# A graph layer's kernel: the node group that is not full comes first, the last groups' products may end behind the last edge tiles, and a piece of the node table per two edge tiles

## The chip, the core and the metric

The kernel runs on one core of a Trainium2 chip. A core has five engines with a program each: PE (TensorE, matrix products), DVE (VectorE), ACT (ScalarE), POOL (GpSimd) and SP (SyncE, which here only issues transfers). They run at the same time and wait for each other by semaphores; each works through its own program in order. Matrix products land in PSUM, everything else on the chip is in SBUF, and transfers (DMA) go between SBUF and the memory outside, HBM. The metric is the time of one launch on the device in microseconds (us).

## What is computed

There are 12500 nodes with 256 features, and 212500 edges, sorted by their target node, each of one of 8 types. Every node has an edge to itself.

```python
h = jnp.maximum(_layernorm(x, axis=-1), 0.0)
hx = jnp.einsum('ni,rio->rno', h, weight)            # 8 weights of 256 x 256
msg = hx[edge_type, src]
agg = jax.ops.segment_sum(msg, dst, num_segments=num_nodes)
node_repr = agg * ALPHA ** 0.5 + h_bias + (h @ loop_weight) * (1.0 - ALPHA) ** 0.5
x = x + node_repr
```

## The kernel before

The kernel sums first and multiplies afterwards: for each target node and type it sums the rows h of the sources, and multiplies these eight sums by the eight weights.

**Edge tiles.** The edges are cut into 802 units, each of two tiles of up to 128 edges (1603 tiles, NT). A unit of blocks 1 and later takes 267 edges; the self edges, each the last of its node's, are taken out of it and treated apart. 128 units are a block (b = 0 to 6). For each tile POOL gathers the 128 source rows from HBM into `msg` (`gather`, L687, its transfer at L704), 58 tiles ahead (AHEAD); some odd tiles are fetched row by row by the queues of SP and ACT instead (L715). DVE makes a one-hot matrix `oh` of (node in a window of 22, type) for four tiles at once (L732). PE multiplies `msg` by `oh` into a PSUM bank `ps` (`edge_sums`, L759), one bank per unit and four banks in all, and DVE adds the bank into `acc` (`add_sums`, L771), one unit later.

**The ring.** `acc` is a ring of 6 x 128 node columns (RING = 768, SLOTS = 6 groups of GROUP = 128) with 8 types each. Where a unit's window lies in it is computed on the chip from its first node: `places` (L581) counts how often the ring has turned by then (`wraps`, L982) and the result is loaded into DVE's registers for 16 units at a time (`load_offsets`, L740, whose DVE load the trace shows at L743), in every 32nd tile.

**Groups.** 128 nodes in order are a group (98 of them; the last has 84 nodes). When the unit that surely holds a group's last edge has been added (`plan.last`), the group's work is put into a queue: eighteen products (L923: the self product with `wl`, then two halves for each of eight types; each product is two passes on PE) into one of two PSUM tiles `po`, and then `finish` (L931), in which DVE adds `x` and the bias and the result (L934, L935), and SP stores it. Four groups (XG) share a tile of rows that is loaded (`load_groups`, L871) and stored at once. A freed slot of the ring is cleared (`clear`, L781) or started with the self edges' terms (`begin`, L806). For the latter, `mark` (L820) and its followers find the type of each node's self edge from the blocks that may hold it (`plan.blocks`).

**The order.** The order of every engine's program is written out by hand in the loop over tiles (L1070 to L1133). In each tile it issues: the gather for 58 tiles on, two single-row fetches per queue, a block's index preparation when it is due (`blocks_ahead`, L1041, in tile 256 b - 184: SP loads the indices, and DVE works on them in the same and the following tiles, its first instruction on them being L381), the rest of what an earlier tile began (`after`), then the edge products, waiting background work, group products from the queue, and the sums of the unit before. The queue's pace comes from a due time: an item has a tile from which it may be issued (`ready`) and one by which it shall be (`until`, L1122), and every tile takes so much from the front that all will be kept.

**The head.** The normalised table h must first be written to HBM: 26 pieces of up to 512 rows are loaded (L672), normalised in `moments` (L644: DVE's statistics, ACT's root at L653, DVE's reciprocal and shift, ACT's activation at L661) and stored (L681), all transfers on SP. Four pieces are begun ahead of the loop. Until the table is there, tiles gather raw rows of x and normalise their messages in the same way, four tiles (BATCH) at once. In the loop (L1079 to L1094) every fourth tile begins a batch of messages and each of the other three begins one piece. When the last piece is done, `norms_end` (L1035) loads the weights, which ACT scales six tiles later (L1031, L1032), and gathers of tiles from 58 + 8 on read h. No group's work is queued before the weights are scaled.

Of the kernel before, what the change touches and what calls it, by code (L numbers as in the profile page):

```python
# [75 lines left out]
class Plan:  # L76
# [7 lines left out]
    def __init__(self, N, E):  # L84
        U = PAIR * P
        first = P * U
        self.NU = NU = -(-E // U) if E <= first else P + -(-(E - first) // EDGES)
        self.EU = E - (NU - 1) * U if E <= first else E - first - (NU - P - 1) * EDGES
        self.NT = NU * PAIR - (1 if self.EU <= P else 0)
        self.rate = N / E * EDGES  # L90
        s = 6.5 * (E / 4) ** 0.5 + EDGES

        lines = [(U, 0), (EDGES, first - P * EDGES)]
        last = (1.1 * EDGES, 1.1 * (first - P * EDGES) - 0.1 * E - 1.5 * EDGES + s)
        self.low = [(a * N / E, (b - s) * N / E) for a, b in [*lines, last]]
        self.high = [(a * N / E, (b + s) * N / E) for a, b in lines]
        self.starts = list(range(0, N, GROUP))
        self.ends = self.starts[1:] + [N]
        self.NG = len(self.starts)
        self.last = [  # L100
            min([NU - 1, *(int((e + 2 - b) / a) + 1 for a, b in self.low)]) for e in self.ends]
        self.last[-1] = NU - 1
        self.first = [
            max(0, min(int((s - WIN - 2 - b) / a) for a, b in self.high) - 1) if s else 0
            for s in self.starts]

        self.blocks = [
            [k for k in range(1, -(-NU // P))
             if max(a * P * k + b for a, b in self.low) <= e + 2
             and max(a * min(NU - 1, P * k + P - 1) + b for a, b in self.high) + WIN + LASTS + 2 >= s]  # L110
            for s, e in zip(self.starts[::XG], self.starts[XG::XG] + [N])]
        self.typed = min([q for q, b in enumerate(self.blocks) if b], default=len(self.blocks))
        assert XG * self.typed >= SLOTS
# [102 lines left out]
def kernel(  # L216
# [48 lines left out]
    ones_b = const.tile([P, P], BF16, name="ones_b")  # L265
    zero = const.tile([P, 1], F32, name="zero")
    flag = const.tile([1, 1], I32, name="flag")
    NK = -(-N // RING)
    wraps = const.tile([P, NK], F32, name="wraps")

    def place_of(t):
# [4 lines left out]
    with ExitStack() as main:  # L276
# [304 lines left out]
        def places(b, got):  # L581

            def wraps_():
                got["wrapped"] = small.tile([P, NK], F32, name="wrapped")
                nc.vector.tensor_scalar(
                    got["wrapped"], wraps, got["base"][:, 0:1], None, op0=ALU.is_lt)

            def turns():
                got["turns"] = small.tile([P, 1], F32, name="turns")
                nc.vector.tensor_reduce(got["turns"], got["wrapped"], AX.X, ALU.add)  # L590

            def position():
                got["pos"] = small.tile([P, 1], F32, name="pos")
                nc.vector.scalar_tensor_tensor(
                    got["pos"], got["turns"], float(-RING), got["base"][:, 0:1],
                    op0=ALU.mult, op1=ALU.add)

            def turn():
                pt = ps_d.tile([P, 512], F32, tag="pt", name="ptr")
                nc.tensor.transpose(pt[0:1, :P], got["pos"], ident)  # L600
                place[b] = small.tile([1, P], I32, name="offs")
                nc.vector.tensor_copy(place[b], pt[0:1, :P])

            return [wraps_, turns, position, turn]
# [266 lines left out]
        def load_groups(name, table, q):  # L871

            if XG * q >= plan.NG:
                return
            d0, d1 = plan.starts[XG * q], plan.ends[min(plan.NG, XG * (q + 1)) - 1]
            full, rest = divmod(d1 - d0, P)
            rows_ = got[name, q] = rowp.tile([P, XG, D], F32, tag="rows", name=f"{name}r")
            if full:
                nc.sync.dma_start(
                    rows_[:, :full, :],  # L880
                    table[d0 : d0 + full * P].rearrange("(k p) d -> p k d", p=P))
            if rest:
                nc.sync.dma_start(rows_[:rest, full, :], table[d0 + full * P : d1])

        def group_ahead(g):

# [23 lines left out]
        def group_work(g):  # L910

            d0, n = plan.starts[g], plan.ends[g] - plan.starts[g]
            s0 = g % SLOTS * GROUP
            first_dep = [True]

            def product(r, c):
                if (r, c) == (R, 0):
                    got["out", g] = outs[g % 2][:, 0, :]
                if r == R:
                    lhs, rhs = got["self", g][:, c, :n], wl[:, c, :]  # L920
                else:
                    lhs, rhs = acc[:, c, r, s0 : s0 + n], w[:, c, r * D : (r + 1) * D]
                i = nc.tensor.matmul(got["out", g][:n], lhs, rhs, start=(r == R and c == 0),  # L923
                                     stop=(r == R - 1 and c == KC - 1))
                if (r, c) == (R, 0) and g < 2:
                    tc.add_manual_dep(i.ins, done["bias"], SYNC_DEP, reason="one engine at a time")
                if r < R and first_dep[0]:
                    first_dep[0] = False
                    tc.add_manual_dep(i.ins, added[plan.last[g]].name, SYNC_DEP, reason="sums complete")

            def finish():  # L931
                q, k = divmod(g, XG)
                rows_ = got["x", q]
                nc.vector.tensor_add(rows_[:n, k, :], rows_[:n, k, :], outs[g % 2][:n, 1, :])  # L934
                nc.vector.tensor_add(rows_[:n, k, :], rows_[:n, k, :], got["out", g][:n])  # L935
                if XG * (q + 1) >= plan.NG:
                    nc.sync.dma_start(out[d0 : d0 + n], rows_[:n, k, :])
                elif k == XG - 1:
                    first = plan.starts[XG * q]
                    nc.sync.dma_start(  # L940
                        out[first : d0 + n].rearrange("(k p) d -> p k d", p=P), rows_)
                b = g + SLOTS
                q, k = divmod(b, XG)
                if b < plan.NG:
                    if q < plan.typed:
                        clear(b)
                    else:
                        begin(b)
                if q + 1 >= plan.typed and XG * (q + 1) < plan.NG:
                    if k == XG // 4:  # L950
                        load_groups("h", h32, q + 1)
                    if k == XG - 2:
                        mark(q + 1)
                    if k == XG - 1:
                        done["late"].append((done["tile"] + REST, lambda: find_types(q + 1)))
                        done["late"].append((done["tile"] + 2 * REST, lambda: spread_types(q + 1)))

            def last():
                done["late"].append((done["tile"] + REST, finish))

            work = []
            for r in [R, *range(R)]:
                for c in range(KC):
                    work.append((0.55, lambda r=r, c=c: product(r, c)))
            work.append((0.0, last))
            return work

        with tc.manual_schedule():
# [10 lines left out]
            tid = small.tile([P, NB], I32, name="tid")  # L979
            nc.gpsimd.iota(tid, pattern=[[P, NB]], base=0, channel_multiplier=1)  # L980
            for k in range(NK):
                nc.gpsimd.memset(wraps[:, k : k + 1], (k + 1) * RING - 0.5)  # L982
            nc.vector.memset(eps, EPS)
            nc.vector.memset(ones, 1.0)
            nc.vector.memset(ones_b, 1.0)
# [84 lines left out]
            for t in range(NT):  # L1070
# [7 lines left out]
                after = []  # L1078
                if t % BATCH == BATCH - 1:  # L1079
                    after = batch(t + 1 + BATCH)  # L1080
                elif done["norm"] < len(pieces):
                    for i in range(1 if NT > 400 else 20):
                        if done["norm"] < len(pieces):
                            after.append(norm_rows(done["norm"]))
                            done["norm"] += 1
                    if NT <= 400:
                        for f in after:
                            f()
                        after = []
                    if done["norm"] == len(pieces):  # L1090
                        for f in after:
                            f()
                        after = []
                        norms_end(t)  # L1094
# [19 lines left out]
                while waiting and (len(waiting) > LAG or t == NT - 1):  # L1114
                    u, ps = waiting.pop(0)
                    add_sums(u, ps)
                    while (next_group < plan.NG and plan.last[next_group] <= u
                           and (done["weights"] or (NT <= 400 and done["norm"] == len(pieces)))):
                        g = next_group
                        while background and NT <= 400:  # L1120
                            background.pop(0)[1]()
                        until = PAIR * (plan.first[g + SLOTS] - 3) - REST if g + SLOTS < plan.NG else NT - 1  # L1122
                        ready = t + max(0, min(DELAY, NT - 1 - t - 2 * DELAY))
                        until = max(ready, min(until, ready + int(GROUP / plan.rate * PAIR)))
                        if g and g % SLOTS == 0:
# [44 lines left out]
```

## Time and profile before

| what | before |
|---|---|
| median of 3 runs | 2582.19 us (2568.44, 2582.19, 2586.18) |
| profiled execution | 2603.5 us, its span 2601.8 us |
| mean granted clock of PE | 0.889 |
| PE, POOL, DVE, ACT busy | 1956.1, 1491.8, 1322.9, 219.5 us |
| gathers from x, from h | 96, 1475 |
| first, last gather from h begins | 178.8, 2519.4 us |
| tile 8, 28, 40, 56 begins on PE | 100.8, 158.5, 189.3, 212.3 us |
| tile 72, 96, 120, 1602 begins on PE | 236.4, 277.3, 306.9, 2586.4 us |
| last store issued | behind 2597.6 us |

The profile is of one execution, and its engines' busy times are sums over a span in which several work side by side. PE's matmuls are pipelined, so the distance from one start to the next says more than a duration. A tile's four passes on PE are those of L759; the n-th tile's start was counted off from them. "Idle before" names what ended an engine's wait; the word issue there means that no wait for another engine is seen.

### The profile page before, as it was taken

What the parts mean: (1) busy time and instruction counts of PE and PEld (TensorE: products, weight loads), DVE (VectorE), ACT (ScalarE), POOL (GpSimd) and SP (SyncE); (2) the same over time, 40 slices, a digit from 0 to 9 for tenths busy, and PEclk for the clock granted to TensorE, in tenths of its full rate; (3) what the DMA queues carried; (4) which work ended last, traced back from release to release, by engine and by line L of the source; (5) the groups of instructions that cost most, each with busy time, mean ns of one, the idle gap of its engine ahead of it and who ended that gap; (6) DMA issues with size and microseconds to landing.
All of it is one profiled execution on the core that took longest, in us unless ns stands there. A gap on an engine that the chain in (4) does not pass through costs nothing. (4 is left out here: it accounts for less than half of the span.)

```text
span 2601.8 us, 42363 instructions
## 1 busy us (share of the span) xinstructions
PE 1956.1 (75%) x10411; PEld 1733.3 (67%) x10411; DVE 1322.9 (51%) x3281; ACT 219.5 (8%) x470; POOL 1491.8 (57%) x1597
## 2 busy tenths in 40 slices
PE   0248887876788777878777777878688787787888
PEld 0237776775677666767666676767577676676778
DVE  3577644455645344754444744444745444744453
ACT  3564100000000000000000000000000000000000
POOL 7435666655566565566566565666466665565640
PEclk9558989988989898889998898999798998898999
DMA  6682433333333333233333233333333333333320
GB/s 198 203 280 83 121 90 115 106 92 110 96 96 106 99 105 111 86 112 104 94 114 110 84 105 109 96 104 98 96 106 94 114 104 86 108 106 92 111 79 13
DMA packets 153661, 282.02 MB, mean 108 GB/s; under 512 B 31709, under 2 KB 103140, under 8 KB 153412
## 3 DMA queue, kind: packets, MB, share of 16 engines
q0 software_dynamic: 75408, 206.01, 27.4%
q1 hardware_dynamic: 73908, 71.16, 8.7%
q10 hardware_dynamic: 4096, 2.11, 0.3%
q8 instruction: 86, 1.41, 0.2%
q14 instruction: 163, 1.34, 0.2%
HBM read 253.55 MB, written 25.60 MB: 107 GB/s over the span
## 5 line engine op out<-in xcount | busy, mean ns | idle before, releaser
L704 POOL DMA_INDIRECT msg<-h,gidx x1475 | 1398.9, 948 | 943.2 <-issue 359.0
L759 PE MATMUL ps<-oh,msg 128*128 128x176 f32 (+1 forms) x6412 | 1235.0, 323 | 384.3 <-issue 246.2
L759 PEld LDWEIGHTS ps<-oh,msg 128*128 128x128 f32 x6412 | 1117.9, 208 | 532.2 <-issue 307.5
L923 PE MATMUL po<-w,acc 128*128 128x256 f32 x3136 | 959.8, 406 | 51.1 <-issue 50.4
L923 PEld LDWEIGHTS po<-w,acc 128*128 128x128 f32 x3136 | 574.4, 204 | 116.9 <-issue 92.3
L732 DVE TENSOR_TENSOR oh<-fixed,cols 128x704 f32<-128x704 f32 x402 | 355.5, 885 | 512.0 <-remote 242.1
L771 DVE TENSOR_TENSOR acc<-acc,ps 128x352 f32 x802 | 412.9, 515 | 346.6 <-PE ps L759 159.5
L814 DVE SCALAR_TENSOR_TENSOR acc<-types,pst 128x256 f32<-128x256 bf16 (+1 forms) x688 | 234.7, 414 | 148.5 <-remote 99.1
L802 ACT ACTIVATE self_t<-pst 128x256 f32<-128x256 f32 x98 | 37.4, 382 | 1984.3 <-DMA msg<-h 810.3
L704 POOL DMA_INDIRECT msg<-in_x_dram,gidx x96 | 90.9, 947 | 84.6 <-issue 60.8
L923 PE MATMUL po<-wl,self_t 128*128 128x256 f32 x392 | 113.6, 409 | 16.6 <-issue 12.5
L923 PEld LDWEIGHTS po<-wl,self_t 128*128 128x128 f32 x392 | 72.9, 206 | 30.5 <-issue 21.5
L840 PE MATMUL ptt<-loops,mark 128*128 128x24 bf16 x216 | 9.3, 177 | 94.3 <-ACT self_t L802 59.5
L840 PEld LDWEIGHTS <-mark 128*128 128x128 bf16 x216 | 9.0, 100 | 97.9 <-issue 97.7
L661 ACT ACTIVATE xt<-xt,n_shift,n_rstd 128x256 f32<-128x256 f32 x98 | 50.9, 589 | 21.2 <-DVE n_shift L658 6.9
L661 ACT ACTIVATE msg<-msg,e_shift,e_rstd 128x256 f32<-128x256 f32 x96 | 49.8, 589 | 17.2 <-DVE e_shift L658 6.0
L795 PE MATMUL pst<-ident,hr 128*128 128x128 f32 x196 | 42.3, 293 | 10.6 <-issue 8.1
L934 DVE TENSOR_TENSOR xr<-xr,po 128x256 f32<-128x256 f32 x98 | 40.4, 412 | 19.1 <-remote 11.5
L935 DVE TENSOR_TENSOR xr<-xr,po 128x256 f32<-128x256 f32 x98 | 41.2, 421 | 3.4
L356 DVE TENSOR_SCALAR moves<-fixed 128x267 int32<-128x267 int32 x84 | 36.3, 432 | 1.6
L858 ACT ACTIVATE diagonal<-ident,kinds 128x128 bf16<-128x128 f32 x88 | 28.1, 390 | 104.8 <-DVE kinds L855 42.9
L795 PEld LDWEIGHTS pst<-ident,hr 128*128 128x128 f32 x196 | 27.9, 152 | 13.5 <-issue 10.4
(201 smaller groups left out, 382.8 us busy)
## 6 DMA issues: line engine op xcount, KB each, us to landing
msg<-h SPq DMA_DIRECT2D x2048, 1.0 KB
msg<-h ACTq DMA_DIRECT2D x2048, 1.0 KB
msg<-h,gidx POOLq DMA_INDIRECT x1475
xt<-in_x_dram SPq DMA_DIRECT2D x24, 512.0 KB
h<-xt SPq DMA_DIRECT2D x24, 512.0 KB
xr<-in_x_dram SPq DMA_DIRECT2D x24, 512.0 KB
hr<-h SPq DMA_DIRECT2D x24, 512.0 KB
out_dram<-xr SPq DMA_DIRECT2D x24, 512.0 KB
```

Of the source, the lines that this page charges most:

```text
L356: nc.vector.tensor_single_scalar(m, packed, 1 << (bit + k), op=ALU.bitwise_and)
L661: nc.scalar.activation(rows_[j], rows_[j], AF.Relu, bias=shift[:n, j : j + 1], scale=rstd[:n, j : j + 1])
L704: nc.gpsimd.indirect_dma_start(out=msg[t], out_offset=None, in_=table[:, :], in_offset=bass.IndirectOffsetOnAxis(ap=gidx[b][:, at : at + 1 ...
L732: nc.vector.tensor_tensor(o[:, k : k + v, :i, :], iota_f.unsqueeze(1).unsqueeze(1).to_broadcast([P, v, i, C]), of.unsqueeze(3).to_broadcas ...
L759: nc.tensor.matmul(ps[:, c, from_ : from_ + width], m[:, c * P : (c + 1) * P], o[:, :width], start=(i == 0 and c == 0), stop=(end and c == ...
L771: i = nc.vector.tensor_tensor(a, a, ps, op=ALU.add)
L795: nc.tensor.transpose(pst[:, c, :n], rows_[:n, c * P : (c + 1) * P], ident[:n, :n])
L802: i = nc.scalar.activation(got["self", g][:, :, :n], pst[:, :, :n], AF.Copy)
L814: i = nc.vector.scalar_tensor_tensor(acc[:, :, r, s0 : s0 + n], of, float(r + 1), pst[:, :, :n], op0=ALU.is_equal, op1=ALU.mult)
L923: i = nc.tensor.matmul(got["out", g][:n], lhs, rhs, start=(r == R and c == 0), stop=(r == R - 1 and c == KC - 1))
L934: nc.vector.tensor_add(rows_[:n, k, :], rows_[:n, k, :], outs[g % 2][:n, 1, :])
L935: nc.vector.tensor_add(rows_[:n, k, :], rows_[:n, k, :], got["out", g][:n])
```

## The change

Three things are done. First, the group of 84 nodes becomes group 0 (nodes 0 to 83), and all later groups are full: every boundary moves by `pad` = 44 nodes. In the ring, node d stands at (d + 44) mod 768, so group 0 takes columns 44 to 127. `wraps_` and `position` compute that place with the same number of instructions. The first four groups' rows are loaded in two transfers and stored group by group; the last two are loaded in one. Second, the groups whose products have no later slot to clear are due at tile NT + 2 and not at NT - 1. Third, a piece of the node table is begun in every even tile that begins no batch, so in two of four tiles, and not in three of four.

```diff
-        self.starts = list(range(0, N, GROUP))
+        self.pad = -N % GROUP
+        self.starts = [0, *range(GROUP - self.pad, N, GROUP)]
...
-    NK = -(-N // RING)
+    NK = -(-(N + plan.pad) // RING)
...
                 nc.vector.tensor_scalar(
-                    got["wrapped"], wraps, got["base"][:, 0:1], None, op0=ALU.is_lt)
+                    got["wrapped"], wraps, got["base"][:, 0:1], float(-RING),
+                    op0=ALU.is_lt, op1=ALU.mult)
...
                 nc.vector.scalar_tensor_tensor(
-                    got["pos"], got["turns"], float(-RING), got["base"][:, 0:1],
-                    op0=ALU.mult, op1=ALU.add)
+                    got["pos"], got["turns"], float(plan.pad), got["base"][:, 0:1],
+                    op0=ALU.add, op1=ALU.add)
...
-            d0, d1 = plan.starts[XG * q], plan.ends[min(plan.NG, XG * (q + 1)) - 1]
-            full, rest = divmod(d1 - d0, P)
+            gs = range(XG * q, min(plan.NG, XG * (q + 1)))
             rows_ = got[name, q] = rowp.tile([P, XG, D], F32, tag="rows", name=f"{name}r")
-            if full:
+            first = gs[0]
+            if plan.ends[first] - plan.starts[first] < P:
                 nc.sync.dma_start(
-                    rows_[:, :full, :],
-                    table[d0 : d0 + full * P].rearrange("(k p) d -> p k d", p=P))
-            if rest:
-                nc.sync.dma_start(rows_[:rest, full, :], table[d0 + full * P : d1])
+                    rows_[: plan.ends[first], 0, :], table[: plan.ends[first]])
+                first += 1
+            k = first - gs[0]
+            if k < len(gs):
+                nc.sync.dma_start(
+                    rows_[:, k : len(gs), :],
+                    table[plan.starts[first] : plan.ends[gs[-1]]].rearrange("(k p) d -> p k d", p=P))
...
-            s0 = g % SLOTS * GROUP
+            s0 = (d0 + plan.pad) % RING
...
-                if XG * (q + 1) >= plan.NG:
+                if q == 0 or XG * (q + 1) >= plan.NG:
                     nc.sync.dma_start(out[d0 : d0 + n], rows_[:n, k, :])
...
-                nc.gpsimd.memset(wraps[:, k : k + 1], (k + 1) * RING - 0.5)
+                nc.gpsimd.memset(wraps[:, k : k + 1], (k + 1) * RING - plan.pad - 0.5)
...
                 if t % BATCH == BATCH - 1:
                     after = batch(t + 1 + BATCH)
-                elif done["norm"] < len(pieces):
+                elif t % 2 == 0 and done["norm"] < len(pieces):
...
-                        until = PAIR * (plan.first[g + SLOTS] - 3) - REST if g + SLOTS < plan.NG else NT - 1
+                        until = PAIR * (plan.first[g + SLOTS] - 3) - REST if g + SLOTS < plan.NG else NT + 2
```

## The prediction

> **What bounds the kernel now.** I read the page's busy table and slices first, then the three stretches head, middle and tail, then the chain at the end. The profiled execution took 2603.5 us (span 2601.8); the median of the three runs shown is 2582.2, so the sum below is made on the trace and its difference is then taken off the median.
>
> ```profile
> PE   0248887876788777878777777878688787787888
> DVE  3577644455645344754444744444745444744453
> POOL 7435666655566565566566565666466665565640
> PEclk9558989988989898889998898999798998898999
> ```
>
> No engine is full in the middle; PE is nearest, at 7 to 8 tenths. The first three slices (195 us) are another stage: PE is nearly idle there, and its clock is at 0.5. The same stage by stretches (columns: us, busy us of PE, weight load, DVE, ACT, POOL, granted clock, DMA share):
>
> ```profile
> 100.80:172.00 71.20, 32.33 (x104) 28.00 (x104) 55.43 (x255) 58.54 (x124) 22.67 (x24) 0.50 0.90 297
> 172.00:189.30 17.30, 6.18 (x25) 5.65 (x25) 7.95 (x29) 7.66 (x12) 7.56 (x8) 0.60 0.91 290
> 236.40:277.30 40.90, 28.70 (x150) 24.85 (x150) 35.77 (x114) 15.50 (x28) 25.80 (x27) 0.87 0.31 88
> 2519.40:2603.00 83.60, 37.26 (x216) 34.44 (x216) 0.99 0.07 22
> ```
>
> (The last line is of the edge products, L759, alone.) From 100.8 to 172 ACT is busy 82% and DVE 78%: they normalise the node table and the first messages in turn, and this is the bound there. From 172 to 189 ACT waits for the weights. From 236 to 277 DVE is busy 87%, because the messages that are still raw are normalised beside the index work of block 1. After POOL's last gather (2519.4) PE has 216 passes of edge products left, 54 tiles, and works without a gap: the tail.
>
> ```profile
> 138.20 2.07 ACT L661 ACTIVATE xt<-xt,n_shift,n_rstd 128x256 f32<-128x256 f32 x4 [0.44 <-DVE n_shift L658]
> 140.18 0.28 ACT L653 ACTIVATE n_rstd<-n_mv,eps 128x4 f32<-128x4 f32 x1
> 141.28 2.08 ACT L661 ACTIVATE xt<-xt,n_shift,n_rstd 128x256 f32<-128x256 f32 x4 [0.82 <-DVE n_rstd L657]
> 143.98 2.07 ACT L661 ACTIVATE xt<-xt,n_shift,n_rstd 128x256 f32<-128x256 f32 x4 [0.44 <-DVE n_shift L658]
> ...
> 146.69 1.09 ACT L661 ACTIVATE msg<-msg,e_shift,e_rstd 128x256 f32<-128x256 f32 x2 [0.44 <-DVE e_shift L658]
> ```
>
> The head's cadence: every group of four rows, a piece of the table (xt) or a batch of messages (msg), costs 2.7 us on the ACT-DVE round trip, 3.1 once in four tiles (the one-hots get in). Three pieces and one batch per four tiles are 11.2 us.
>
> ```profile
> 2586.43 0.76 PE L759 MATMUL ps<-oh,msg 128*128 128x176 f32 x4
> 2588.68 1.06 PE L923 MATMUL po<-wl,self_t 128*84 128x256 f32 x4 [1.49 <-DVE xr L935]
> 2589.58 7.07 PE L923 MATMUL po<-w,acc 128*84 128x256 f32 x32
> ```
>
> The end: after the last tile PE waits 1.49 us, then does 36 passes of the last group's products.
>
> **The change part by part**
>
> *A. Half the pieces per tile.* Before, pieces go on three of four tiles, so the 22 that are left when the loop starts end at tile 28; after, on two of four, at tile 42. Messages are gathered raw for tiles up to the end of the pieces + 58 + 8: 96 before, 108 after, so three more batches. In time: batch 8 has one piece fewer ahead of it, 100.2 - 2.7 = 97.5. Then nine rounds of four tiles at 2 pieces + 1 batch = 8.5 us, two of them with a clear (0.9 more): 78.3. The two short pieces end it at 181.8, against 172.0. So the table ends 10 us later, but PE's supply is at tile 48 and not at 34. The weight loads are queued on SP behind the last stores, and their scaling ended 16.0 us after the table (188.0 - 172.0): 197.8 after. Tiles up to 55 need nothing behind that scaling, so PE begins tile 56 at about 199.1; before, it began tile 40 at 189.3. No group's products have been done at either point: both wait for the scaled weights.
>
> Then the catching up. A pass of an edge product is 0.15 us apart (0.6 a tile), one of a group product 0.215, 36 to a group.
> Tiles 56 to 72: before 24.1 us (16 x 0.6 + 36 x 0.215 + 6.4 of stall while DVE loads its registers, L743). After, groups 0 and 1 both fall here (order of the built program: 56 to 62, 62 to 71): 7.7 more, 31.8; at tile 72 after stands at 230.9, before at 236.4.
> Tiles 72 to 96: before 40.8, DVE bound; after 24 more passes, 5.2 us of PE, of which I put 2 on the path, since PE idles 12 us there.
> Tiles 96 to 120: before 29.7. After, 12 of these tiles are raw too. A raw tile makes DVE's load about 1.7 us (from the 40.8 for 24 tiles) where the others go by in 1.25: +5; 14 group passes fewer: -3, partly hidden: +3 net.
> Sum at tile 120: 230.9 + 42.8 + 32.7 = 306.4, against 306.9: **-0.5 us**. The trace doesn't show this mix. Bounds: if PE's own work set the pace from tile 56, 64 x 0.6 + 180 x 0.215 + 13 for two register loads = 90, tile 120 at 289, -18; if none of the lead is kept and the later end of the table and three batches count whole, 10 + 5 = +15. I take the value by stretches, nearest to the rows.
>
> *B. The short group first.* Every group boundary but the last comes 44 nodes earlier, 2.8 units, 5.6 tiles. Number of groups and products is the same (98 x 36 passes; the width moved is 256 for the short group too). So work moves earlier: behind tile 1545, where PE is at POOL's last gather, 108 products stand before and 102 after; 12 passes x 0.215 = **-2.6**, done earlier where PE has idle time (bounds -2.6 and 0).
> The last group has 128 rows instead of 84. The row first: 32 passes with 84 weight columns take 7.07 us, 18 with 128 take 4.05; without the last pass's 0.38 both are 0.216 apart, though one weight load falls from 190 to 153 ns. The Trainium skill, "TensorE: Matmul & The Clock Gate", section LDWEIGHTS, makes a weight load proportional to its columns: 44/1.2 = 37 ns, which the two rows confirm for the load alone, and which would speak against this change by 36 x 37 ns = 1.3 us at the very end. The passes hide it: 0.
>
> *C. Products may end behind the last tile* (due NT + 2 for NT - 1). In the built order, five products of group 96 and the two self products of group 97 now stand behind the last edge tile: 14 passes, 3.0 us, more than the 1.49 us that PE waits for DVE's last sums and the release of its output bank: **-1.5** (bounds -1.5 and 0).
>
> *D. What rows 0 to 3 cost on the queues.* They are loaded in two transfers each (x and h) and written in four, so SP issues two more loads and three more stores. Row: a 512 KB store holds SP 0.4 us. [...] nothing on an engine waits for these stores, so 0 directly. But SP's order changes: the store of group 0 now stands ahead of the loads of rows 4 to 7 and of block 1's indices. Before, SP got through all these at 177 to 188 us, and DVE found the indices at 236.9 without waiting. After, SP waits for group 0's last addition, then issues 0.4 + 2.2 + 1.9 + 1.6 + 0.7 us (the durations of 177.7 to 187.2) and the load lands some 2 us later: 9 us. DVE has about 8 us of work between that addition and its first index instruction, so it waits 1: **+1**. Bounds: 0, and the waits at the five later blocks, 7 to 18 us.
>
> *E. Small.* One more block mark (28 for 27): two DVE instructions of 0.48, eight PE passes of 0.18, half on the path: **+1**. The multiply in the wrap count and the other constants add no instruction. At blocks 5 and 6 a store and a load change places around the index loads on SP: block 5, which waits longest now (17.9), loses them, block 6 gets them: 0 (bounds -8, +8).
>
> Sum: -0.5 - 2.6 - 1.5 + 1 + 1 = -2.6 us; against the profiled execution 2600.9, against the median **2579**.
>
> **The rivals**
>
> *The lead is kept whole* (A at its low bound). For it: PE is idle 12 of 41 us at tiles 72 to 96. Against: DVE is at 87% there, and gets three more batches. Then -18 - 2.6 - 1.5 + 2 = -20: 2562.
>
> *DVE makes it slower.* Mechanism: the catching up doesn't happen, since from tile 56 to 108 DVE carries raw batches, two groups' additions and, from tile 72, block 1; the 10 us by which the table ends later stay, with the three batches. Place: tiles 56 to 108. Price: +15 - 4 + 2 = +13, 2595; with a wait of 18 us for block 1's indices (D's upper bound) +31, 2613. It decides from the point where tile 72 falls later than 236.4 us in the trace, that is where tiles 56 to 72 take over 37 us.
>
> *It doesn't do what it says:* the steady middle is paced by PE with DVE's stalls (index loads 56 us, register loads), and moving a group boundary against them by 5.6 tiles shifts single stalls by some us, either way. Then the sum is lost in it: 2582 +- 8.
>
> **How the numbers follow.** My forecast (-10 to +4 on the median) has 0.50, the lead kept whole 0.12, DVE slower 0.24, the shifted stalls 0.14. About 1% (26 us) can be told from no change by a measurement of this kernel; the three runs shown lie 18 us apart. Under 2556 only the second case with that spread comes: 0.08. Over 2608 the third with the index wait: 0.17. The rest, 0.75, is within. The predicted time is that of the first case, 2579. For 8 in 10: from 2558 (the lead kept, a few us of spread) to 2606 (DVE slower, most of the index wait).
>
> **What would show it.** The last piece's activation near 182 us and tile 56 near 199; groups 0 and 1 back to back with PE full; tile 72 near 231 and 120 near 306; no gap between the last edge product and the end of PE; DVE's first index instruction without a long wait. It is wrong if tile 120 is off by over 10 us, if the middle's pace (tile 120 at 306.9, tile 1549 at 2519.6: 1.55 us a tile) changes by over 1%, or if block 1's indices make DVE wait.

## The result and the profile after

| | before | after |
|---|---|---|
| median (22 runs each, one chip) | 2577.41 us (2567.33 to 2590.52) | 2593.39 us (2575.64 to 2615.32) |
| ratio, 95% interval | | 1.0054 (1.0037 to 1.007) |
| profiled execution, its span | 2603.5, 2601.8 us | 2575.6, 2573.9 us |
| tile 8, 40, 52, 56 begins | 100.8, 189.3, 208.4, 212.3 us | 96.2, 170.5, 191.6, 207.5 us |
| tile 72, 96, 120 begins | 236.4, 277.3, 306.9 us | 233.4, 271.9, 305.9 us |
| tile 1549 begins, from there to the end | 2519.6, 82.2 us | 2497.0, 76.9 us |

The change makes the kernel slower by 0.54%, some 14 us. The two profiles say the opposite: the profiled execution of before was above all its timed runs, that of after was the fastest of its own. So these two traces can be compared by stage, head against head, but not by their ends.

In the changed file a line of before stands two to six lines further down (L759 is L762, L661 is L664, L923 is L929). The page's slices of after:

```profile
PE   1357787886877877888877787887687788687889
...
PEclk9558898998998988989989888889898998898999
```

The head is busier (PE's first three slices are 1, 3, 5 for 0, 2, 4), the middle is as before. By stretches (columns as before: us, busy us of PE, weight load, DVE, ACT, POOL, granted clock, DMA share, GB/s):

```profile
96.20:184.70 88.50, 48.98 (x158) 42.68 (x159) 69.94 (x308) 68.27 (x144) 38.49 (x42) 0.50 0.82 261
184.70:207.50 22.80, 10.14 (x42) 8.76 (x42) 14.79 (x55) 13.61 (x26) 9.79 (x11) 0.65 0.72 222
207.50:233.40 25.90, 25.90 (x143) 22.92 (x142) 15.12 (x55) 12.05 (x24) 13.03 (x14) 0.97 0.40 125
233.40:271.90 38.50, 29.48 (x158) 26.39 (x157) 36.45 (x119) 14.44 (x27) 23.99 (x26) 0.91 0.32 94
271.90:305.90 34.00, 27.19 (x149) 24.48 (x150) 20.69 (x64) 8.58 (x16) 17.07 (x19) 0.90 0.39 120
```

From 207.5 to 233.4 PE is full (25.90 of 25.90, clock 0.97): the catching up of groups 0 and 1 in tiles 56 to 72. Before it stand 22.8 us in which PE works 10.14. What ACT did in them (start, duration, instruction):

```profile
184.14 0.60 ACT L664 ACTIVATE xt<-xt,n_shift,n_rstd 84x256 f32<-84x256 f32 x1 [0.42 <-DVE n_shift L661]
...
186.47 2.07 ACT L664 ACTIVATE msg<-msg,e_shift,e_rstd 128x256 f32<-128x256 f32 x4 [0.44 <-DVE e_shift L661]
...
190.04 2.07 ACT L664 ACTIVATE msg<-msg,e_shift,e_rstd 128x256 f32<-128x256 f32 x4 [0.44 <-DVE e_shift L661]
193.25 1.91 ACT L1037 ACTIVATE w<-w 128x2048 f32<-128x2048 f32 x1 [1.13 <-DMA w<-in_L_gnn_weight_dram]
195.06 0.40 ACT L1038 ACTIVATE wl<-wl 128x256 f32<-128x256 f32 x1
199.39 1.91 ACT L1037 ACTIVATE w<-w 128x2048 f32<-128x2048 f32 x1 [3.93 <-issue]
201.21 0.40 ACT L1038 ACTIVATE wl<-wl 128x256 f32<-128x256 f32 x1
```

The table's last activation (xt) begins at 184.14, and then two raw batches and the four scalings stand in ACT's order. PE's program has group 0's first work before tile 56, and so PE stops:

```profile
189.71 4.47 PE L762 MATMUL ps<-oh,msg 128*128 128x176 f32 x23
202.42 0.54 PE L798 MATMUL pst<-ident,hr 84*128 84x84 f32 x2 [8.24 <-DMA hr<-h]
205.66 2.00 PE L929 MATMUL po<-wl,self_t 128*84 128x256 f32 x4 [2.70 <-ACT self_t L805]
207.46 1.38 PE L762 MATMUL ps<-oh,msg 128*128 128x176 f32 x4
```

From tile 52 (191.6) to tile 56 (207.5) PE loses 8.24 us on the row load of group 0 and 2.70 on ACT's copy. A lead of 16.9 us at tile 52 is 4.8 at tile 56. The end of the trace:

```profile
2557.72 0.76 PE L762 MATMUL ps<-oh,msg 128*128 128x176 f32 x4
2558.31 2.32 PE L929 MATMUL po<-w,acc 128*128 128x256 f32 x10
2560.47 1.03 PE L929 MATMUL po<-wl,self_t 128*128 128x256 f32 x4
2561.33 7.07 PE L929 MATMUL po<-w,acc 128*128 128x256 f32 x32
```

No gap is left between the last edge product and the end: ten passes of group 96 and the self products cover what was a wait of 1.49 us.

### The profile page after: what moved, and what is told of

Same layout as the page of the kernel before. It is cut to its first block, busy times and chain, and to the rows that moved or that the text cites. A ratio compares the mean times of both kernels' runs of the same rounds, so it can differ in the third digit from the quotient of the medians.

```text
span 2573.9 us, 42430 instructions
## 1 busy us (share of the span) xinstructions
PE 1952.0 (76%) x10419; PEld 1738.7 (68%) x10419; DVE 1331.3 (52%) x3313; ACT 226.9 (9%) x485; POOL 1493.5 (58%) x1597
## 5 line engine op out<-in xcount | busy, mean ns | idle before, releaser
L762 PE MATMUL ps<-oh,msg 128*128 128x176 f32 (+1 forms) x6412 | 1242.7, 325 | 365.9 <-issue 221.1
L762 PEld LDWEIGHTS ps<-oh,msg 128*128 128x128 f32 x6412 | 1125.0, 209 | 507.8 <-issue 328.5
L929 PE MATMUL po<-w,acc 128*128 128x256 f32 (+1 forms) x3136 | 955.3, 406 | 51.6 <-issue 50.4
L929 PEld LDWEIGHTS po<-w,acc 128*128 128x128 f32 (+1 forms) x3136 | 575.6, 204 | 108.5 <-issue 84.8
L774 DVE TENSOR_TENSOR acc<-acc,ps 128x352 f32 x802 | 411.8, 514 | 319.2 <-PE ps L762 161.3
L817 DVE SCALAR_TENSOR_TENSOR acc<-types,pst 128x256 f32<-128x256 bf16 x688 | 235.0, 412 | 146.5 <-remote 99.5
L805 ACT ACTIVATE self_t<-pst 128x256 f32<-128x256 f32 (+1 forms) x98 | 37.5, 383 | 1962.9 <-DMA msg<-h 670.9
L929 PE MATMUL po<-wl,self_t 128*128 128x256 f32 (+1 forms) x392 | 108.3, 399 | 5.0 <-ACT self_t L805 2.7
L929 PEld LDWEIGHTS po<-wl,self_t 128*128 128x128 f32 (+1 forms) x392 | 70.7, 200 | 12.2 <-issue 3.4
L664 ACT ACTIVATE msg<-msg,e_shift,e_rstd 128x256 f32<-128x256 f32 x108 | 56.0, 589 | 19.7 <-DVE e_shift L661 8.9
L798 PE MATMUL pst<-ident,hr 128*128 128x128 f32 (+1 forms) x196 | 40.3, 285 | 18.3 <-issue 10.1
L664 ACT ACTIVATE xt<-xt,n_shift,n_rstd 128x256 f32<-128x256 f32 x98 | 50.9, 588 | 19.5 <-DVE n_shift L661 8.0
L940 DVE TENSOR_TENSOR xr<-xr,po 128x256 f32<-128x256 f32 (+1 forms) x98 | 40.4, 412 | 22.9 <-remote 9.6
L798 PEld LDWEIGHTS pst<-ident,hr 128*128 128x128 f32 (+1 forms) x196 | 26.7, 147 | 25.3 <-issue 16.7
L941 DVE TENSOR_TENSOR xr<-xr,po 128x256 f32<-128x256 f32 (+1 forms) x98 | 41.2, 420 | 3.4
L652 DVE BATCH_NORM_STATS2 e_stats<-msg 128x6 f32<-128x256 f32 x108 | 37.7, 410 | 0.0
```

The source lines that it names most:

```text
L652: nc.vector.bn_stats(stats[:n, j, :], rows_[j])
L664: nc.scalar.activation(rows_[j], rows_[j], AF.Relu, bias=shift[:n, j : j + 1], scale=rstd[:n, j : j + 1])
L762: nc.tensor.matmul(ps[:, c, from_ : from_ + width], m[:, c * P : (c + 1) * P], o[:, :width], start=(i == 0 and c == 0), stop=(end and c == ...
L774: i = nc.vector.tensor_tensor(a, a, ps, op=ALU.add)
L798: nc.tensor.transpose(pst[:, c, :n], rows_[:n, c * P : (c + 1) * P], ident[:n, :n])
L805: i = nc.scalar.activation(got["self", g][:, :, :n], pst[:, :, :n], AF.Copy)
```

## The experiments

Five chips were used, each with before beside the kernels. On one of them before takes 2013 us (chip A here), on the others 2580 to 2608, near the 2577 of the comparison above. Times are medians of 13 to 22 runs (e2 and e4: five, e17: six, e16: eight); the ratios to before, with their 95% intervals, are not quotients of the medians.

| run | edit | before | time | ratio |
|---|---|---|---|---|
| e1_groups | group shift alone | 2013.17 | 2012.79 | 1.0001 (0.9993 to 1.001) |
| e2_pace | pace alone | 2013.17 | 2024.1 | 1.0057 (1.0043 to 1.007) |
| e3_due | due time alone | 2013.17 | 2011.08 | 0.9993 (0.9985 to 1.0001) |
| e4_again | whole change | 2013.17 | 2023.76 | 1.0055 (1.0041 to 1.0069) |
| e5_late20 | 12 more raw tiles | 2579.88 | 2586.41 | 1.0023 (1.0008 to 1.0038) |
| e6_wearly | weights loaded early | 2579.88 | 2584.41 | 1.0 (0.9975 to 1.0025) |
| e7_pace_wearly | pace, weights early | 2579.88 | 2575.79 | 0.9978 (0.9963 to 0.9993) |
| e8_fast2 | two pieces in three of four tiles | 2579.88 | 2590.32 | 1.0041 (1.0026 to 1.0056) |
| e9_pace | pace alone | 2607.81 | 2608.8 | 0.9996 (0.9978 to 1.0014) |
| e10_pace_scale14 | pace, weights scaled later | 2607.81 | 2601.36 | 0.9973 (0.9954 to 0.9992) |
| e11_scale14 | weights scaled later | 2607.81 | 2603.11 | 0.9976 (0.9954 to 0.9999) |
| e12_after_wearly | whole change, weights early | 2607.81 | 2616.53 | 1.0032 (1.0013 to 1.0052) |
| e13_groups | group shift alone | 2608.28 | 2618.89 | 1.0044 (1.0024 to 1.0064) |
| e14_after | whole change | 2608.28 | 2618.75 | 1.0033 (1.0013 to 1.0054) |
| e15_due | due time alone | 2608.28 | 2605.53 | 0.9986 (0.9967 to 1.0004) |
| e16_groups_delay12 | group shift, work 6 tiles later | 2608.28 | 2595.36 | 0.9949 (0.9928 to 0.997) |
| e17_before_delay0 | before, work 5 tiles earlier | 2603.8 | 2633.9 | 1.0111 (1.0072 to 1.0151) |
| e18_before_delay12 | before, work 6 tiles later | 2603.8 | 2608.4 | 1.0015 (0.9997 to 1.0034) |

**The three parts one by one.** e1 is the changed kernel with pace and due time put back, e2 and e3 are before with one line each, e4 is the changed kernel.

```diff
e1, against after
-                elif t % 2 == 0 and done["norm"] < len(pieces):
+                elif done["norm"] < len(pieces):
...
-                        until = ... else NT + 2
+                        until = ... else NT - 1
e2, against before
-                elif done["norm"] < len(pieces):
+                elif t % 2 == 0 and done["norm"] < len(pieces):
e3, against before
-                        until = ... else NT - 1
+                        until = ... else NT + 2
```

> The short group first alone: pieces on three of four tiles and the old due time, as before. Theory G (moving every group boundary by 5.6 tiles against the fixed tiles of the index and register loads costs the time in the middle): +10 to +16 us against before, like the whole change. Theory P (the slower pace of the table's pieces costs it): -4 to 0 us. Theory S (the shift, the pace and the due time each cost little and only together show): +3 to +6.

> Before with one line changed: a piece of the table in two of four tiles. Theory G: -5 to +3 us against before, with tile 56 some 5 us earlier and tile 120 within 3 us of before. Theory P: +10 to +16 us. Theory S: +3 to +6.

> Before with one number changed: the last groups are due at NT + 2. Theories G and P alike: -2 to 0 us, the gap of 1.5 us ahead of the last group's products gone. Theory D (more products left behind the last edge tile lengthen the end): +2 to +5 us.

> The whole change once more, for a second profile and to see how far single executions lie apart. All theories: +10 to +18 us against before in the median. If its profile is a longer one than the first (2575.6 us), the difference between the two profiles by stretches of tiles shows where the kernel's own spread lies; theory G expects it between tiles 120 and 1545.

On this chip the whole cost is the pace's: e2 and e4 are both 11 us slower, e1 is not, and the due time (e3, 2 us faster by the medians) is not told from zero by its interval. The trace of e2 shows the place: PE from tile 54 on.

```profile
134.34 1.32 PE L759 MATMUL ps<-oh,msg 128*128 128x176 f32 x8 [0.36 <-DVE acc L771]
147.84 0.69 PE L795 MATMUL pst<-ident,hr 128*128 128x128 f32 x2 [12.18 <-DMA hr<-h]
149.27 2.07 PE L923 MATMUL po<-wl,self_t 128*128 128x256 f32 x4 [0.74 <-ACT self_t L802]
151.13 1.38 PE L759 MATMUL ps<-oh,msg 128*128 128x176 f32 x4
```

Tile 52 begins at 132.7 in e2 and at 149.9 in e3, tile 56 at 151.1 and 153.8: a lead of 17 us shrinks to 3 while PE waits 12.18 us for group 0's rows. Then 7 us are lost in tiles 56 to 72, in which two groups are caught up (23.4 us in e2, 16.7 in e3), and 7 in tiles 96 to 120 (35.9 for 29.1), half of which are still raw in e2. Tile 120 comes at 247.7 in e2 against 237.1 in e3. The middle (tiles 130 to 1545) is the same in all four, 1671.1 to 1672.7 us.

**What the pace costs, and what the weights do.** The first comparison was on a chip like the other four, so the head was taken apart on such chips. e5 makes the same number of raw tiles without the pace, e6 loads the weights eight pieces before the table's end, e7 does so with the pace, and e8 makes the table end earlier.

```diff
e5
-LATE = 8
+LATE = 20
e6 and e7 (e7 has the pace of e2 too)
-                load_weights()
...
+                            if done["norm"] == len(pieces) - 8:
+                                load_weights()
e8
-                    for i in range(1 if NT > 400 else 20):
+                    for i in range(2 if NT > 400 else 20):
```

> Before with LATE = 20 for 8: twelve more tiles gathered raw (108 for 96), the table's pace as before. Theory R (the three more raw batches at tiles 96 to 108 cost the time, because DVE is the bound there): +8 to +11 us, the whole of the pace's cost. Theory W (the wait for the weights swallows the lead) and theory T (each batch that is put ahead of the table's end delays it by 3 us and gives PE only 2.4 us of work): +2 to +5.

> Before with the weights' load issued eight pieces ahead of the table's end; scaling in the same tile as before. All theories: the wait of ACT for the weights (some 12 us between message batches 36 and 40) shrinks to 3 or less, and the kernel gains 6 to 11 us, because PE stands idle in it.

> The pace of two in four tiles, with the weights' load issued eight pieces ahead of the table's end. Theory W: without the wait the lead of 14 tiles is kept, so this is not slower than e6_wearly: -5 to 0 us against it. Theory T: it stays 8 to 12 us slower than e6_wearly, as the pace is slower than before. Theory R: 8 to 11 slower too, with the difference arising between tiles 96 and 108.

> Before with two pieces in each of three of four tiles: the table ends at tile 15 or so and 80 tiles are gathered raw. Theory T: four batches of 3 us fewer ahead of the table's end, and 16 x 0.6 us less of PE's work done by then: -2 to -6 us against before, unless the transfers, at 0.98 of their share from 100 to 150 us in the trace of before, set the table's pace; then 0 to +4. Theory W: the lead was worth nothing, so the table's earlier end counts whole: -8 to -12.

Three more raw batches cost 6.5 us (e5), which lies between the two expectations and decides for neither. Ending the table earlier (161.6 us in e8, for 172.0) does not help: tile 56 comes at 219.2, later than in before. Early weights give nothing to before (e6, for an expected gain of 6 to 11 us: the table then ends at 177.7), but with the pace they give a kernel that is 4 us faster than before (e7: tile 56 at 202.6, tile 120 at 299.2).

The next four were run on another chip. Here the scaling is issued 14 tiles behind `norms_end` and not 6 (e10, e11); e12 is the whole change with early weights.

```diff
-                background.append((t + 6, scale_weights))
+                background.append((t + 14, scale_weights))
```

> The pace of two in four tiles alone, again, beside the next three on one chip. All theories: +9 to +16 us against before.

> The pace, with the weights scaled 14 tiles after the table's end and not 6, so that two more message batches stand ahead of the scaling on ACT. Theory W (ACT, and behind it PE, waits for the weights in its order, and the lead of 14 tiles is lost there): tile 56 starts some 10 us earlier than with the pace alone, and the kernel is 6 to 10 us faster than that. Theory T (a batch ahead of the table's end costs more than it gives) and theory C (PE has too much to catch up once the weights are there): within 3 us of the pace alone, or slower, since the products start later.

> Before, with the weights scaled 14 tiles after the table's end. Theory W: the same wait goes from before: 4 to 8 us faster than before. Theory C: 0 to +4.

> The whole change, with the weights' load issued eight pieces ahead of the table's end. Theory W: 15 us faster than the whole change without it, so some 5 us faster than before. Theories T and C: 5 faster than the whole change at most, so still 5 to 10 us slower than before.

Two things follow. Scaling later moves tile 56 from 210.2 (e9) to 195.0 us (e10) and tile 120 from 307.6 to 297.3, so it is what hangs on the weights that swallows the lead. e10 alone can't tell the row load from ACT's order, since group 0's first work, too, then stands behind tile 56. The traces with early weights can. PE before tile 56 in e7:

```profile
194.54 0.38 PE L795 MATMUL pst<-ident,hr 128*128 128x128 f32 x2
200.78 2.07 PE L923 MATMUL po<-wl,self_t 128*128 128x256 f32 x4 [5.85 <-ACT self_t L802]
202.65 1.38 PE L759 MATMUL ps<-oh,msg 128*128 128x176 f32 x4
```

The wait for group 0's rows, 8.24 us in the trace of after, is gone: there SP issued this load at 191.5 us, behind those of the weights, in e7 at 185.9. What stays is ACT's copy behind the raw batches and the scalings, 5.85 us here and 6.89 in e12. So both had a part.

And on this chip the pace alone costs nothing (e9, for an expected 9 to 16 us), while e12 is 9 us slower than before although its head is ahead of e9's (tile 120 at 302.1 for 307.6). So here the cost is behind the head, and neither the pace nor the weights make it.

**The group shift in the middle.** e13 is e1, e14 the changed kernel, e15 is e3, now on a chip on which before takes 2608 us. In e16 the shift stays, but `DELAY`, the tiles between a group's last sums and its products, is doubled.

```diff
e16, against e13
-DELAY = 6
+DELAY = 12
```

> The boundaries of the groups moved by 44 nodes, with the pace and the due time of before, the same kernel as in e1_groups (ratio 1.0001 on a chip on which before takes 2013 us). Theory G (on chips on which before takes 2580 to 2610 us the group shift costs in the middle, tiles 120 to 1545, because the groups' work falls in other tiles): ratio 1.003 to 1.008, +8 to +20 us, and about as slow as e14_after. Theory P (the whole cost is the pace's, here as on the quiet chip): 1.000 +- 0.001. Theory S (a sum of small parts): 1.002.

> The whole change again, beside its parts on one chip. All theories: slower than before by what the first comparison gave, ratio 1.004 to 1.007. Theory G: e13 and e14 within 0.15% of each other. Theory P: e14 slower than e13 by 0.4% or more. If it is within 0.2% of before here, the cost of the change is a matter of the chip.

> Before with only the due time NT + 2. All theories: -1 to -2 us, ratio 0.9995, as in e3_due (0.9993). It also shows what spread there is on this chip between two kernels whose programs are the same up to the last three tiles.

> e13 with the spreading constant DELAY at 12 and not 6, so that the groups' products, which the shift has moved some tiles earlier, come about where they came before the shift. Theory G, because of the tile phase (the products fall beside the tiles in which DVE loads its registers or prepares a block): the cost of e13 goes, ratio 0.998 to 1.001. Theory G, because of anything else (the boundaries themselves, the four separate stores): as e13. Theory P: as e13, near 1.000.

The shift alone costs as much as the whole change (+11 and +10 us). In the traces its groups' first products stand in tiles 53, 69, 87, 103, 121, where before has 59, 75, 93, 109, 127. With `DELAY` 12 they stand in 59, 75, 93, 109, 127 again (79 of the 98 groups in the very tile of before, most others two later), the boundaries still being shifted. The cost is gone, and the kernel is 13 us faster than before. So the boundaries, the separate stores and the constants, which e16 keeps, don't make the cost by themselves: it hangs on when the groups' work falls.

The tail pays: from tile 1549 to the end e14 takes 77.0 us and e16 82.6. The middle gives it back. Of the four, e14 and e16 were profiled near their medians (2622.9 and 2595.8 us; e13 15 us above its own, e15 18 below), so these two are set side by side: first the 48 tiles about block 6 (1336 to 1383), then tiles 130 to 1545, in the columns of above.

```profile
2206.30:2299.80 93.50, 63.16 (x312) 54.70 (x311) 59.90 (x158) 1.54 (x4) 47.68 (x51) 0.84 0.32 91
324.90:2540.00 2215.10, 1730.16 (x9239) 1539.29 (x9238) 1103.17 (x2507) 78.12 (x202) 1315.50 (x1384) 0.89 0.35 100
```

```profile
2183.00:2268.30 85.30, 60.82 (x313) 54.13 (x313) 55.92 (x147) 1.15 (x3) 45.27 (x49) 0.82 0.33 95
317.30:2507.40 2190.10, 1729.85 (x9236) 1535.92 (x9235) 1103.24 (x2505) 78.11 (x202) 1315.42 (x1384) 0.88 0.35 102
```

Over the whole middle the busy times of PE, DVE and POOL agree within 1 us, and e14 takes 25 us more: all of the difference is waiting. The stretch about block 6 is 8 us longer in e14: PE is idle for 30.3 us of it (its length less PE's busy time) for 24.5 in e16, and busy for 2.3 us more. PE and DVE there, e14 and then e16, each around the preparation's begin (tile 1352):

```profile
2237.42 0.59 PE L929 MATMUL po<-w,acc 128*128 128x256 f32 x2
2248.52 0.44 DVE L383 TENSOR_TENSOR rise<-nat_d 128x267 f32<-128x267 int32 x1 [15.38 <-DMA nat_d<-in_dst_dram]
...
2250.06 0.51 DVE L774 TENSOR_TENSOR acc<-acc,ps 128x352 f32 x1
...
2250.68 1.51 PE L762 MATMUL ps<-oh,msg 128*128 128x176 f32 x4 [12.66 <-issue]
...
2259.16 0.41 PE L345 MATMUL ptr<-ident,sf 128*128 128x128 f32 x2 [3.13 <-DVE sf L410]
```

```profile
2210.55 1.03 PE L929 MATMUL po<-w,acc 128*128 128x256 f32 x4
2218.10 0.44 DVE L383 TENSOR_TENSOR rise<-nat_d 128x267 f32<-128x267 int32 x1 [12.98 <-DMA nat_d<-in_dst_dram]
...
2219.71 0.51 DVE L774 TENSOR_TENSOR acc<-acc,ps 128x352 f32 x1
...
2220.32 1.51 PE L762 MATMUL ps<-oh,msg 128*128 128x176 f32 x4 [8.74 <-issue]
...
2225.53 1.51 PE L762 MATMUL ps<-oh,msg 128*128 128x176 f32 x4 [1.04 <-issue]
2232.17 0.66 PE L345 MATMUL ptr<-ident,sf 128*128 128x128 f32 x2 [5.12 <-DVE sf L410]
```

The last bracket is the idle time. The trace gives "issue" for PE's longest stop (12.66 and 8.74 us), so it names no releaser. But in both kernels PE goes on 0.1 us after DVE has added a bank to `acc` (L774), and in DVE's order this addition stands behind the wait for the block's indices (15.38 and 12.98 us). So this stop hangs on the indices. It isn't the 8 us, though: PE's stops in these lines sum to 15.8 us in e14 and 14.9 in e16, and the rest lies elsewhere in the stretch.

The 48 tiles about each of the blocks 2 to 6 (from 16 ahead of the preparation to 32 behind its begin, 240 tiles in all) sum up as follows, counted from the tiles' starts on PE:

| chip (time of before) | work in the tiles of before, or later | work 4 to 6 tiles earlier |
|---|---|---|
| first comparison (2577) | before 435.1 | after 438.8 |
| 2607.81 | e9 439.3, e10 437.9, e11 443.6 | e12 450.3 |
| 2608.28 | e15 429.1, e16 435.1 | e13 455.9, e14 456.7 |
| 2603.8 | e18 428.9 | e17 450.2 |
| 2013.17 (chip A) | e2 358.8, e3 359.9 | e1 369.0, e4 367.8 |

On every chip the work that comes earlier makes these tiles slower, by 4 to 28 us; without chip A the means are 435.6 and 450.4. A part of it is more work: with the shift 1579 of PE's passes fall into the windows, with the order of before 1560, some 4 us by the 0.215 us of a group pass (an estimate). The other tiles from 130 to 1545 show no such difference on these chips (1756.3 and 1754.9 in the mean, single traces up to 23 us off). On chip A the windows cost 9 us as well, but there the other tiles give 10 back (1313.2 and 1303.0), and nothing is left of it in the whole. The windows were chosen after the traces of the slower chips had been read, and a single trace strays by some us, so this points to the place and doesn't prove it. DVE's own wait for the indices is at most a part: over blocks 2 to 6 it sums to 54.1 us in the mean of nine profiles with the boundaries and `DELAY` of before (40.2 to 61.4; chip A is left out) and to 58.9 in the four with the shift (46.3 to 65.8), but to 57.4 in e16.

SP's order changes with the groups' work, too. In e13 the store and the row load of a group stand ahead of block 6's index loads (issued at 2250.2 and 2250.7, the first of these at 2257.8), in e15 and e16 behind them (2219.5 behind 2211.3, 2222.4 behind 2215.3). So e16 puts back both the tiles and this order, and doesn't tell their costs apart.

The last two take the shift away and move the work alone.

```diff
e17
-DELAY = 6
+DELAY = 0
e18
-DELAY = 6
+DELAY = 12
```

> Before with the spreading constant DELAY at 0 and not 6: the groups keep their boundaries, but their products and what goes with them come six tiles earlier, in the tiles in which they come after the change (e13: 53, 69, 87, 103, 121, ...). Theory F (the tiles in which the groups' work falls carry the cost, whatever the boundaries): ratio 1.003 to 1.006, as e13. Theory S (the boundaries themselves, the four separate stores, the one more mark): 1.000 +- 0.0015.

> Before with DELAY at 12, so that the groups' work comes six tiles later than in before (65, 81, 99, ...). Theory L (what counts is the distance between a group's last sums and its products, later is better, and e16 gained by that): ratio 0.991 to 0.996, as far below before as e16 is below e13. Theory F with the tiles of before as good ones: not below 0.999, since the work leaves them. In between: both have a part.

Theory S falls with e16 already. Theory L falls with e18: later work gains nothing by itself (+0.15%, its interval holds 1). Theory F expected 0.3 to 0.6% of e17, and it was 1.1%: the sign is right, but e17 tells less than it should. Its groups' first products stand in tiles 54, 70, 88, 104, 122, one behind those of e13. What the products' matmuls waited for (us, times), in e17 and then in e15:

```profile
  DVE acc L771: 107.8, 25
  issue: 83.3, 86
```

```profile
  issue: 65.4, 111
  ACT self_t L802: 2.4, 1
```

At `DELAY` 0 a group's products come so soon behind its last sums (L771) that they wait for them, 25 times, which e15 doesn't know. So e17 has a cost of its own besides that of the tiles.

What stays open: why e16 is 13 us below before, though most of their products stand in the same tiles (0.998 to 1.001 was expected, it was 0.9949), while e18 has the same constant and gains nothing; which of the instructions that meet in the tiles about a block preparation cost the time; and why chip A wins it back elsewhere. No run tells these apart. e16 (2595.36 us) beats before (2608.28) and the changed kernel (2618.75) on the same chip, on eight runs.

## Why the forecast was wrong, step by step

**The head (A) was right in sum and wrong in its steps.** Tile 120 was forecast at 306.4 us and came at 305.9. The table's last activation ended at 184.7 (forecast 181.8: the round of four tiles took about 9.1 us and not 8.5), the scaling at 201.6 (197.8). Tile 56 came at 207.5 and not 199.1: the forecast let PE run to it as soon as the weights were there, and left out that PE's order has group 0's transposes and self product ahead of it, which wait for a row load and for ACT. Tiles 56 to 72 then took 25.9 us and not 31.8, since PE was busy for all of them: the stall of 6.4 us, carried over from before, is not there. Tiles 72 to 96 took 38.5 and not 42.8, tiles 96 to 120 34.0 and not 32.7. That these errors cancel to half a microsecond is luck. e9 confirms the sum on a chip like the first (0.9996); on chip A the same step costs 11 us (e2). One reading of the rows was wrong as well, without weight in the sum: the clock of 0.5 holds for the second and third slice, the first shows 0.9.

**The step that failed is B.** It said that twelve passes move from the tail, "done earlier where PE has idle time (bounds -2.6 and 0)". The tail did get shorter, by 5 us (76.9 for 82.2; 77.0 in e14 for 81.8 in e15). But the place to which the work moves is not free: nearly every group comes four to six tiles earlier, not only the last, and e13 measured the whole shift at +10.6 us (1.0044), outside both bounds. The forecast read PE's seven to eight tenths in the middle as room; e16, with e18 beside it, shows that it hangs on when the work comes, and the tiles about the block preparations are where the traces show it. The last rival named this mechanism, "moving a group boundary against them by 5.6 tiles shifts single stalls by some us, either way", but took it as a spread of 8 us about zero, with a chance of 0.14. That term was mis-sized. For the chip of the first comparison this is an inference: on the chip of e13 and e14 the shift accounts for the whole cost, on that of e12 the cost is behind the head as well, and before has its time and its waits in common with the first chip (2608 and 2577 us), which it hasn't with chip A.

**C** came as forecast as far as it can be seen: -1.5 forecast, -0.07% in e3 (1.4 us) and -0.14% in e15, neither told from zero by its interval; the gap of 1.49 us at the end is gone. **D** was wrong by its 1 us: DVE found block 1's indices without a wait, since SP issued store, loads and indices within 3.2 us (220.9 to 224.1; the forecast summed 6.8), and DVE came to them at 231.4. **E**'s swap shows at block 6, where the four profiles with the shift wait 9.6 to 16.2 us (4.1 to 9.6 in the nine of before's order); at block 5 the ranges overlap (7.7 to 15.4 for 9.2 to 17.9). Blocks 2 and 3, of which the forecast said nothing, changed too: 13.8 to 21.1 for 5.5 to 12.1, and at most 5.4 for 5.9 to 12.4.

The last group's 44 columns more cost nothing, as the forecast took it: its last 32 passes take 7.07 us at the end, with 128 weight columns as with 84, where the rule in the Trainium skill, "TensorE: Matmul & The Clock Gate", section LDWEIGHTS, that a weight load's time goes with its columns, would by itself have added 1.2 us (an estimate from that page: 32 times 44/1.2 ns).

**The rivals.** The lead was not kept whole; DVE didn't make the head slower either (tiles 56 to 72 took 25.9 us, its point was 37). The total, slower by 14 us, looks like that rival's 13 and has nothing to do with it.

## What to carry to other kernels

Work that is moved out of the tail into a middle that isn't full can still cost time, though the mean there is below 100%: look where it lands against the periodic work (index preparation, register loads), and try the landing place by itself with a delay constant before judging the change that moved it. A lead in the head is worth what the next in-order step lets through; here weights in the order of ACT and a row load took 12 us of it within four tiles. Take a change of three parts apart on the kind of chip on which it was measured: the part that costs may be another one on another chip.

## What the runs showed of the hardware

The same kernel took 2013 us on one chip and 2577 to 2608 on the others. The head is the smaller part of that: tiles 130 to 1545 take 1672.4 us in e3, 2194.2 in the profile of before, 2178.2 in e15, with a mean granted clock of 0.952, 0.889 and 0.887. What the others have and chip A lacks is in the list of waits (engine, line, what it waited for: us in all, times, longest). First before, then e3:

```profile
POOL msg L704 <- remote: 260.8, 170, 2.4
...
DVE oh L732 <- remote: 242.1, 75, 6.0
...
DVE acc L771 <- remote: 116.2, 44, 4.6
...
DVE rise L381 <- DMA nat_d<-in_dst_dram: 56.1, 5, 17.9
```

```profile
POOL msg L704 <- issue: 409.0, 1324, 4.5
...
DVE oh L732 <- PE ps L759: 320.0, 222, 3.5
...
DVE acc L771 <- PE ps L759: 156.2, 163, 4.3
...
DVE rise L381 <- DMA nat_d<-in_dst_dram: 24.9, 5, 7.3
```

Waits for which the trace finds no releaser on this core (it prints "remote") hold DVE and POOL for 619 us in these three lines of before, and no wait of e3 has that releaser. It isn't a change of names alone: by the pages, all idle time ahead of the three is 1802 us in before and 960 in e3. The waits for indices fall from 56.1 to 24.9 us. One edit can change its verdict with that: the pace is 1.0057 on chip A and 0.9996 on another, the shift 1.0001 and 1.0044. What the remote cause is, no run here shows.
